# Two lanes of cells and queries that keep their results in DRAM, cross attention two sequences behind, inner products read from DRAM

## The chip, the cores and the metric

The kernel runs on one core of one Trainium2 chip. The metric is the device time in microseconds; the time of a kernel is the median of its runs. Less is better.

## The reference

Eight sequences of 512 tokens with 256 features go through two layers. Every `x = x + tanh(g) * f(layernorm(x))` is a stage. All arithmetic is float32.

```python
# _mlstm_cell: 8 heads of 32, gated and causal
log_D = where(tril, cs[:, :, None] - cs[:, None, :], -inf) + ig[:, None, :]
max_log_D = max(log_D, -1)
C = (q @ k.T) / sqrt(32) * exp(log_D - max_log_D)
h = (C / (maximum(abs(C.sum(-1)), exp(-max_log_D)) + EPS)) @ v
...
x = x + tanh(g_xattn[0]) * cell(layernorm(x), ctx, ctx)        # then layernorm(h) * ln_scale
x = x + tanh(g_ffn[0])   * block2(layernorm(x))                # 32 heads of 8, then 8 experts of 1024
x = x + tanh(g_xattn[1]) * cross(ctx, ctx, layernorm(x))       # 16 heads of 16
x = x + tanh(g_ffn[1])   * peer(layernorm(x))                  # product keys: 4096 experts, 8 of them per head
```

`block2` attends from all 512 tokens to all 512 (softmax), projects, adds, and sends fixed groups of tokens through their experts (gelu). `cross` attends from the sequence to its context. `peer` scores 2 x 64 sub-keys, takes the top 8 of the pairs, and weighs the chosen experts' `gelu(x . down)` by a softmax before the product with `up`. Its batch norm takes mean and variance over all tokens, so the scores of `peer` need every sequence to have passed cross attention.

## The kernel before

The kernel has two phases. `attention_phase` does cell, block 2 and cross attention for all sequences, and the inner products of all 4096 experts with seven of the eight sequences. What follows (`fold_phase` and the loop over `steps` at the end) does the product keys. The change is inside the attention phase.

The backbone of the attention phase is a list of 24 score jobs: for each place m in `order` two jobs of block 2, `("A", m, 0)` and `("A", m, 1)` with 16 heads each, and one of cross attention, `("C", m, 0)`. A job has 16 steps (4 groups of heads by 4 chunks of 128 tokens). It goes through the steps twice: first `maxima` computes queries by keys and takes the negated row maxima (L405, on DVE), which go as one more row into the queries' operand; then `exponentials` computes the transposed scores with the maxima already in, ACT takes the exponential (L433), and `values` multiplies by the value operand (L448). The loop at the end of the phase takes one step of the maxima of one job and one step of the exponentials of an earlier job together, where both are ready: the products of the two stand side by side in the program, on different rows of the array (L387). If one of the two isn't ready, the step is made with the other alone; if neither, the step is empty.

All else is side work in lanes, Python generators that yield either the cost in microseconds of the products that they have just issued, or a condition: `("wait", t)`, `("rest", event)`, `("take", True)` for the one shared accumulator bank (tag `ac`). `beside(credit)` is called twice a step and lets lanes issue until the credit is used up, in a fixed order of preference. So TensorE's order is the order in which this planner calls the instructions (it is set by hand for TensorE alone); the orders on DVE, ACT, GpSimd (POOL) and the sync engine's queue (SP) are made by the framework's scheduler from it.

```python
LAG, CREDIT, GROUP, RETURN = 2, (1.3, 2.4), 1.1, 2.6
jobs += [("A", m, 0), ("A", m, 1)]
if 0 < m < M - 2:
    jobs.append(("C", m - 1, 0))
lanes = [Lane(g()) for g in (between, after, before, behind, fill)]
```

The lanes: `before` runs `cell(m)` and `queries(m)` for all m in turn. A cell loads x into `qn` and the context into `cT` and `cte` (L515 to L518, DMAs issued by POOL), normalizes and transposes, makes the gates and their running sums in rows of 8 x 512, stores the running maximum to DRAM (`nM_d`, L562) and, for each of four pairs of heads, loads it back spread over all partitions (`mb`, L583), masks it (L591 on POOL), takes the exponential (L599, ACT) and multiplies scores (L621), decay (L626, DVE) and values (L606). `queries` projects queries and keys of block 2 and stores them to DRAM (`qk_d`). `between` spreads them into one of three operand sets (L357) and projects the values into `v0` in SBUF. `behind` does output projection, experts, operands and values of cross attention; `after` adds the cross attention, stores the stream and its transpose to DRAM (`x_d`, `xT_d`) and adds to the batch norm's Gram matrix; `fill` makes the inner products (L130), evacuates them (L921) and stores them (`h_d`).

Before, a cell can't begin until its predecessor's queries are done, the stream X of a sequence stands in SBUF from the cell on (three buffers), the values of block 2 can't be projected until `v0` is free, and a job set is given by its half: sets 0 and 1 to the halves, 2 to cross attention.

Of the kernel before, what the change touches and what calls it, by code (L numbers as in the profile page):

```python
# [10 lines left out]
F32 = mybir.dt.float32  # L11
# [10 lines left out]
P = 128  # L22
# [14 lines left out]
def kernel(  # L37
# [52 lines left out]
    def layernorm(dst, src, user):  # L90
# [3 lines left out]
        mv = small.tile([P, NC, 2], F32, name="ln_mv", tag=f"ln_mv{user}", bufs=4 if user == "x" else 1)  # L94
        rs = small.tile([P, NC], F32, name="ln_rs", tag=f"ln_rs{user}", bufs=4 if user == "x" else 1)
# [83 lines left out]
    def attention_phase(ctx: ExitStack):  # L179
# [5 lines left out]
        row = ctx.enter_context(tc.tile_pool(name="row", bufs=1))  # L185
# [17 lines left out]
        gw_sb = row.tile([P, 6, 16], F32, name="gw_sb", tag="cs")  # L203
# [86 lines left out]
        W0, W1, WC = 32 * 9 + 23, 16 * 17 + 15, 8 * 33 + 31  # L290
        v0 = cst.tile([P, NC, W0], F32, name="v0")
        v1 = cst.tile([P, NC, W1], F32, name="v1")
        cte = cst.tile([P, NC, WC], F32, name="cte")
        nc.gpsimd.memset(v0, 1.0)
# [6 lines left out]
        m_f = row.tile([B * NC, P], F32, name="m_f", tag="e")  # L301
# [73 lines left out]
        class Attention:  # L375
# [35 lines left out]
            def close_maxima(self):  # L411
# [6 lines left out]
                nm_sb = row.tile([16, S], F32, name="nm_sb", tag="e")  # L418
# [20 lines left out]
            def values(self):  # L439
# [6 lines left out]
                for j in range(4):  # L446
                    h = (64 * j + self.first) // self.hd + g
# [8 lines left out]
                if self.o is None:  # L456
                    self.o = outs[self.m].setdefault(
                        self.hd, None
                    ) or tok.tile([P, NC, D], F32, name="o", tag="o", bufs=2)
                    outs[self.m][self.hd] = self.o  # L460
# [24 lines left out]
        xbs, cTs, lnx, nTs, qks, xTs, weights = {}, {}, {}, {}, {}, {}, {}  # L485

        def load(m):

            b = order[m]
            xbs[m] = xbp.tile([P, NC, D + 1], F32, name="X")  # L490
            nc.gpsimd.dma_start(xbs[m][:, :, :D], x[b].rearrange("(c p) d -> p c d", p=P))
            nc.gpsimd.memset(xbs[m][:, :, D], 1.0)
            return xbs[m][:, :, :D]
# [6 lines left out]
        def load_expert(n):  # L500
# [3 lines left out]
            nc.gpsimd.dma_start(w1e, w1[e].rearrange("(k p) f -> p k f", p=P))  # L504
            w2e = wmp.tile([P, NF, D], F32, name="w2e", tag="w2e")
# [3 lines left out]
            weights[n] = (e, w1e, w2e, b2e)  # L509


        def cell(m):
            b = order[m]
            qn = trp.tile([P, NC, D], F32, name="qn", tag="t1")
            nc.gpsimd.dma_start(qn, x[b].rearrange("(c p) d -> p c d", p=P))  # L515
            cT = load_context(m, "cTc")
            for c in range(NC):
                nc.gpsimd.dma_start(  # L518
                    cte[:, c, : 8 * 33].rearrange("p (h e) -> p h e", e=33)[:, :, 0:32],
# [1075 lines left out]
```

## Time and profile before

| | |
|---|---|
| median of 3 runs | 4019.05 us (4013.78 to 4032.41) |
| the profiled execution's own time | 4021.59 us |
| its span, first to last instruction | 4019.8 us |
| mean granted TensorE clock | 0.953 |
| TensorE busy | 3602.8 us |
| VectorE, ScalarE, GpSimd busy | 2277.1, 1757.1, 604.4 us |
| first score maximum (L405) | at 156.6 us |
| end of attention, start of the product keys | about 3134 us |

The rows of the profile give busy times by engine; PE is TensorE's matmuls, PEld its weight loads, DVE the vector engine, ACT the scalar engine. A matmul row's duration is modelled, so a busy PE is not PE at its peak. The chain of waits is followed back from the last instruction. "sc" is the tile of scores of both kinds, told apart by the order of its operands: `sc<-ka,qa` are the maxima, `sc<-qa,ka` the exponentials.

### The profile page before, as it was taken

What the parts mean: (1) busy time and instruction counts of PE and PEld (TensorE: products, weight loads), DVE (VectorE), ACT (ScalarE), POOL (GpSimd) and SP (SyncE); (2) the same over time, 40 slices, a digit from 0 to 9 for tenths busy, and PEclk for the clock granted to TensorE, in tenths of its full rate; (3) what the DMA queues carried; (4) which work ended last, traced back from release to release, by engine and by line L of the source; (5) the groups of instructions that cost most, each with busy time, mean ns of one, the idle gap of its engine ahead of it and who ended that gap; (6) DMA issues with size and microseconds to landing.
All of it is one profiled execution on the core that took longest, in us unless ns stands there. A gap on an engine that the chain in (4) does not pass through costs nothing.

```text
span 4019.8 us, 75880 instructions
## 1 busy us (share of the span) xinstructions
PE 3602.8 (90%) x31049; PEld 1861.6 (46%) x31049; DVE 2277.1 (57%) x5581; ACT 1757.1 (44%) x2279; POOL 604.4 (15%) x611
## 2 busy tenths in 40 slices
PE   5587898889989999989998999878899899999998
PEld 2222243334334434433443443423444677777777
DVE  3455564555555555555645553455421679999993
ACT  2124454344544444444444434334344355555562
POOL 3210102011002002100200020010000123333331
PEclk7668999999999999999999999999899999999999
DMA  3201113123213312422232142110333353333331
GB/s 105 53 27 38 27 57 76 43 64 103 83 43 93 106 62 69 122 81 54 72 112 72 51 119 82 41 40 25 113 108 100 96 149 104 103 103 103 112 113 36
DMA packets 200392, 317.53 MB, mean 79 GB/s; under 512 B 24862, under 2 KB 153406, under 8 KB 191742
## 3 DMA queue, kind: packets, MB, share of 16 engines
q1 hardware_dynamic: 183564, 255.74, 21.5%
q0 software_dynamic: 15616, 56.63, 4.7%
q8 instruction: 244, 4.00, 0.4%
q14 instruction: 104, 0.85, 0.1%
q10 hardware_dynamic: 864, 0.32, 0.0%
HBM read 224.08 MB, written 87.72 MB: 78 GB/s over the span
## 4 chain that ended last, share of the span: by engine, by line
PE 78%; DVE 13%; issue 3%; ACT 2%; DMA 2%; POOL 1%; SPq 0%; DVEq 0%; POOLq 0%; ACTq 0%
PE sc L387 22%; PE acc L1437 11%; PE ps_hd L130 10%; DVE nm L405 9%; PE av L448 7%; PE cf L1417 3%; PE ps_y L764 3%; PE ps_sim L1169 3%; PE ps_q L347 3%; PE ps_p L336 3%; PE ps_h L747 3%; PE csc L621 2%; PE cav L606 2%; PE ps_t L317 1%; PE ps_hl L130 1%
## 5 line engine op out<-in xcount | busy, mean ns | idle before, releaser
L405 DVE TENSOR_REDUCE nm<-sc 128x2 f32<-128x1024 f32 x768 | 939.8, 1225 | 1024.6 <-PE sc L387 1021.0
L433 ACT ACTIVATE pr<-sc 128x1024 f32<-128x1024 f32 x768 | 785.8, 1024 | 1034.3 <-PE sc L387 1032.4
L387 PE MATMUL sc<-ka,qa 32*128 32x512 f32 x3072 | 940.8, 673 | 211.7 <-DVE nm L405 199.6
L387 PE MATMUL sc<-qa,ka 32*128 32x512 f32 x3072 | 895.0, 657 | 23.2 <-ACT pr L433 13.7
L387 PEld LDWEIGHTS sc<-ka,qa 32*128 32x128 f32 x3072 | 256.2, 191 | 624.8 <-DVE nm L405 430.6
L1437 PE MATMUL acc<-up_sb,gs 64*128 64x256 f32 x4096 | 468.3, 382 | 1.3 <-DVE gs L1426 1.3
L130 PE MATMUL ps_hd<-xT,dw 128*64 128x256 f32 x3584 | 432.5, 385 | 3.9 <-DVE pd L626 2.1
L448 PE MATMUL av<-pr,v 128*32 128x512 f32 x3072 | 427.3, 629 | 4.7 <-ACT pr L433 4.7
L1437 PEld LDWEIGHTS acc<-up_sb,gs 64*128 64x128 f32 x4096 | 389.8, 187 | 52.4 <-issue 4.7
L130 PEld LDWEIGHTS ps_hd<-xT,dw 128*64 128x64 f32 x3584 | 243.1, 137 | 232.2 <-issue 103.9
L1407 POOL TENSOR_TENSOR m<-o,cwT 128x1024 f32<-128x1024 bf16 x128 | 243.7, 1904 | 561.4 <-DVE o L1405 238.5
L387 PEld LDWEIGHTS sc<-qa,ka 32*128 32x128 f32 x3072 | 241.3, 187 | 68.2 <-issue 32.4
L921 ACT COPY hb<-ps_hd 128x512 f32<-128x512 f32 x224 | 130.9, 586 | 296.2 <-PE ps_hd L130 282.7
L599 ACT ACTIVATE pd<-mb,aT 128x512 f32<-128x512 f32 (+3 forms) x256 | 129.7, 553 | 211.0 <-PE cav L606 95.5
L448 PEld LDWEIGHTS av<-pr,v 128*32 128x32 f32 x3072 | 61.5, 109 | 308.9 <-issue 291.3
L591 POOL TENSOR_SCALAR_AFFINE_SELECT mb<-mb 128x256 f32<-128x256 f32 x128 | 52.4, 409 | 858.4 <-ACT pd L599 410.7
L1426 DVE TENSOR_TENSOR gs<-cf,gs 128x1024 f32<-128x1024 f32 x128 | 155.7, 1217 | 42.7 <-PE cf L1417 27.3
L626 DVE SCALAR_TENSOR_TENSOR pd<-csc,pd 128x512 f32<-128x512 f32 (+3 forms) x256 | 115.5, 485 | 96.0 <-PE csc L621 70.7
L621 PE MATMUL csc<-qT,cT 32*128 32x256 f32 (+3 forms) x512 | 148.1, 557 | 13.7 <-DVE pd L626 10.2
L1417 PE MATMUL cf<-m,m 64*64 64x64 f32 x8192 | 152.5, 221 | 0.8 <-DVE gs L1426 0.7
L1417 PEld LDWEIGHTS cf<-m,m 64*64 64x64 f32 x8192 | 134.8, 135 | 38.7 <-issue 38.3
L1403 ACT CAST m<-o 128x1024 f32<-128x1024 bf16 x128 | 133.6, 1044 | 39.2 <-DVE o L1401 35.4
(225 smaller groups left out, 4081.6 us busy)
## 6 DMA issues: line engine op xcount, KB each, us to landing
h_d<-hb SPq DMA_DIRECT2D x224, 256.0 KB
gs<-h_d SPq DMA_DIRECT2D x56, 1024.0 KB
dw<-in_down SPq DMA_DIRECT2D x112, 256.0 KB
w1e<-in_w POOLq DMA_DIRECT2D x16, 1024.0 KB, 5.4
w2e<-in_w POOLq DMA_DIRECT2D x16, 1024.0 KB, 6.4
mb<-nM_d SPq DMA_DIRECT2D x32, 512.0 KB
qk_d<-pk SPq DMA_DIRECT2D x64, 256.0 KB
ws<-in_w SPq DMA_DIRECT2D x56, 256.0 KB
```

The costliest lines, as they stand in the source:

```text
L130: nc.tensor.matmul(ps[64 * q : 64 * q + 64, :], dw[:, k, :], runs[:, :, q, :], start=(k == 0), stop=(k == NK - 1),)
L387: nc.tensor.matmul(sc[:, i, :], lhs[r : r + 32, g, c * P : (c + 1) * P], rhs[r : r + 32, g, :], start=True, stop=True,)
L405: newest = nc.vector.tensor_reduce(self.nm[:, c, 2 * half : 2 * half + 2, g], sc, AX.X, ALU.max, negate=True)
L433: nc.scalar.activation(self.pr[jj], sc, AF.Exp)
L448: nc.tensor.matmul(self.av[32 * j : 32 * j + 32, :], self.va[:, c, h * (self.hd + 1) : h * (self.hd + 1) + 32], pr[j // 2][:, j % 2, :], s ...
L621: nc.tensor.matmul(sc[i][:, s0:], cT[r : r + 32, g, s0 : s0 + P], qT[r : r + 32, g, s0:], start=True, stop=True,)
L921: nc.scalar.copy(hb.rearrange("p n i t -> p i n t"), ps.rearrange("p i (n t) -> p i n t", n=2),)
L1403: nc.scalar.copy(m1, o1)
L1407: nc.gpsimd.tensor_tensor(m2, o2, tokens(cw), ALU.mult)
L1417: nc.tensor.matmul(cf[64 * q : 64 * q + 64, h, s, :], m2[rows, 4 * q + s // 2, :, s % 2], m1[rows, 4 * q + s // 2, :, s % 2], start=True, ...
L1426: nc.vector.tensor_tensor(gv, cf.rearrange("p h s i -> p i h s"), gv, ALU.mult)
L1437: nc.tensor.matmul(accs[n][q], gs[n % 2][rows, i, :], up_sb[rows, i, :], start=(i == 0), stop=(i == 63),)
```

## The change

Seven things are changed together, all in the attention phase.

1. Cells and queries run in two lanes: one takes sequences 0, 2, 4, 5, 6, 7, the other 1 and 3. The second works in tiles lent by what is not yet in use (`Lent`: the experts' weights and hidden units, and until the first scores the accumulator bank `av`). Before the first scores, the cells' products use the score banks.
2. The cell's result goes to DRAM (`x_d1`), and `behind` loads it as X when its turn comes. The values of block 2 are projected at the end of `queries`, stored to DRAM (`v_d`), and loaded into one of two half-size `v0` before their job.
3. The gates' rows use the cell's tiles `pd` and `mb`; the pool `row` is gone.
4. The cross attention of m-2, not of m-1, stands among the jobs of m, between the two; the three operand sets rotate.
5. The expert weights w1 are loaded when the hidden units are done, w2 and b2 later, and the pause between experts is 3, not 20. The first expert is loaded when the second lane is through.
6. The inner products read the transpose from DRAM (`xT5`) and need no longer share a tile with `leave`.
7. The credits fall from (1.3, 2.4) to (1.1, 2.1).

The core of the diff:

```diff
+        class Tiles:
+            user = ""
...
+            def pair(self):
+                return cel.tile([P, 2, S], F32, name="pd")
+
+            def bank(self, name):
+                return ps_ac.tile([P, S], F32, name=name, tag="ac")
...
+        class Lent(Tiles):
+            user = "2"
+
+            def __init__(self):
+                self.pds = wmp.tile([P, 2, 2, S], F32, name="pd2", tag="heT")
+                self.more = wmp.tile([P, 2, NC, D], F32, name="mb2", tag="w2e")
+                self.cte = wmp.tile([P, NC, WC], F32, name="cte2", tag="w1e")
...
-        def cell(m):
+        def cell(m, own):
...
+                def banks():
+                    if newest:
+                        return [ps_m.tile([P, S], F32, name="csc", tag="m") for _ in range(2)]
+
+                    two = ps_sc.tile([P, 2, S], F32, name="csc2", tag="sc")
+                    return [two[:, i] for i in range(2)]
...
-            yield ("rest", ("left", m - 3))
-            Xb = load(m)
...
-            nc.gpsimd.tensor_tensor(Xb, Xb, hk, ALU.add)
+            nc.gpsimd.tensor_tensor(Xa, Xa, hk, ALU.add)
+            xds[m] = drm.tile([P, NC, D], F32, name="x_d1", bufs=M)
+            nc.sync.dma_start(xds[m], Xa)
...
+            vds[m] = drm.tile([P, 2, NC, 16 * 9], F32, name="v_d", bufs=M)
             w = weights1.get()
             for c in range(NC):
-                ps = project(w, nTs[m], c)
-                nc.any.tensor_copy(
-                    v0[:, c, : 32 * 9].rearrange("p (h e) -> p h e", e=9)[:, :, 0:8],
-                    ps.rearrange("p (h e) -> p h e", e=8),
+                ps = project(w, nT, c)
...
+                nc.sync.dma_start(
+                    vds[m][:, :, c], pk.rearrange("p (f n) -> p f n", f=2)
                 )
                 yield 1.0
+            rested.add(("v_d", m))
...
+        def begin(m):
+            for f in range(2):
+                i, last = block2_set(m, f)
+                yield ("rest", ("qk", m))
+                if last:
+                    yield ("rest", last)
+                for half, src in zip(sets[i], qks[m]):
+                    spread(half, src, 32 * f, 8)
+                blank(sets[i][0])
+                ready.add(("A", m, f))
+                yield ("rest", ("v_d", m))
+                yield ("rest", ("A", m - 1, f))
+                nc.sync.dma_start(v0[f][:, :, : 16 * 9], vds[m][:, f])
+                ready.add(("v0", m, f))
...
+                if 2 * m + i + 1 < 2 * M:
+                    load_first(2 * m + i + 1)
...
                 if i == 0:
-                    yield ("wait", 20)
+                    yield ("wait", 3)
...
         def inner(m):
             b = order[m]
+            xT = exp.tile([P, NK, S], F32, name="xT5", tag="xT5", bufs=1)
+            nc.sync.dma_start(xT, xT_d[:, :, b * S : (b + 1) * S])
+            yield ("wait", 4)
...
-        LAG, CREDIT, GROUP, RETURN = 2, (1.3, 2.4), 1.1, 2.6
+        LAG, CREDIT, GROUP, RETURN = 2, (1.1, 2.1), 1.1, 2.6
...
         for m in range(M):
-            jobs += [("A", m, 0), ("A", m, 1)]
-            if 0 < m < M - 2:
-                jobs.append(("C", m - 1, 0))
+            jobs.append(("A", m, 0))
+            if 1 < m < M - 1:
+                jobs.append(("C", m - 2, 0))
+            jobs.append(("A", m, 1))
...
+        def before(sequences, tiles):
+            own = tiles()
+            for m in sequences:
+                Xa = yield from cell(m, own)
+                yield from queries(m, own, Xa)
+            if tiles is Lent:
+                rested.add("lent")
+                load_first(0)
+                load_second(0)
...
-        lanes = [Lane(g()) for g in (between, after, before, behind, fill)]
+        lanes = [Lane(g()) for g in (between, after)]
+        lanes += [Lane(before((0, 2, *range(4, M)), Tiles)), Lane(behind()), Lane(before((1, 3), Lent))]
+        lanes.append(Lane(fill()))
...
                 if (
                     job not in closed or tick < closed[job] + LAG or value not in ready
-                    or not free
+                    or not free or ("v_d", 1) not in rested
                 ):
```

## The prediction

> **What bounds the kernel now.** I read the page's totals, then a table of busy time by stretch, then the chain of waits inside single stretches. From the page, section 1 and section 4:
>
> ```profile
> PE 3602.8 (90%) x31049; PEld 1861.6 (46%) x31049; DVE 2277.1 (57%) x5581; ACT 1757.1 (44%) x2279; POOL 604.4 (15%) x611
> PE 78%; DVE 13%; issue 3%; ACT 2%; DMA 2%; POOL 1%; SPq 0%; DVEq 0%; POOLq 0%; ACTq 0%
> ```
>
> TensorE bounds the whole, but 90% is a mean. The busy table, with stretches cut where the score jobs change hands (columns: stretch, length, busy time and instructions of PE, weight loads, DVE, ACT, POOL, granted PE clock, DMA share, GB/s):
>
> ```profile
> 0.00:157.00 157.00, 80.75 (x222) 36.43 (x223) 54.69 (x127) 27.43 (x49) 58.95 (x79) 0.67 0.32 92
> 157.00:264.00 107.00, 89.16 (x276) 32.59 (x274) 61.38 (x95) 22.96 (x42) 7.39 (x17) 0.60 0.12 29
> 264.00:504.00 240.00, 192.11 (x1089) 64.55 (x1088) 136.29 (x237) 96.51 (x125) 33.25 (x44) 0.88 0.12 33
> 504.00:768.00 264.00, 232.30 (x1295) 103.64 (x1292) 141.36 (x230) 114.62 (x139) 32.75 (x45) 0.97 0.23 62
> 1101.00:2409.00 1308.00, 1212.01 (x8036) 546.39 (x8032) 705.93 (x1127) 593.73 (x728) 161.57 (x215) 0.99 0.28 81
> 2649.00:2846.00 197.00, 160.06 (x1004) 61.91 (x1000) 100.75 (x122) 86.70 (x87) 6.16 (x8) 0.97 0.09 23
> 3005.00:3134.00 129.00, 124.95 (x862) 61.11 (x858) 17.32 (x49) 55.14 (x71) 3.50 (x6) 1.00 0.35 111
> 3134.00:4019.00 885.00, 854.52 (x13890) 663.13 (x13890) 725.05 (x3143) 457.40 (x677) 247.08 (x130) 0.99 0.33 101
> ```
>
> The reader is to see three things. From 1101 to 2409 PE is 93% busy at full clock: little to win except by taking work out of its steps. Up to 264 PE is 64% busy and that at 0.60 to 0.67 of its clock. And from 2649 to 2846 it has holes, because the side work has run out. After 3134 the product-key phase begins, which the diff does not touch: 885 us stay.
>
> What a step costs is in the chain of 2660 to 2680, where nothing but scores runs:
>
> ```profile
> 2666.32 1.21 PE sc L387 x8
> 2667.54 1.22 DVE nm L405
> 2668.75 0.04 issue
> 2668.80 1.21 PE sc L387 x8
> 2670.01 1.22 DVE nm L405
> ```
>
> Half a step is scores 1.21 plus the maximum 1.22 plus 0.04: 2.47 us, a step 4.94. PE's own part is 2 x 1.21 and 1.00 for the value product (a row "av L448 x8" of 1.00 in the chain): 3.42. A step with scores for the exponentials alone has "sc L387" 1.06 twice and the 1.00: 3.1 us. So a step that carries only one of the two kinds costs PE nearly as much as one with both, since the two kinds use different rows of the array side by side (`jj` and `1 - half` in `pair`).
>
> **What the Trainium skill says.** "TensorE: Matmul & The Clock Gate", Part 1: the clock is halved after an idle window of about 3.4 us and given back after a busy one. The trace agrees in part: half clock up to 264 where PE waits, full clock later; but from 200 to 240 PE counts as 94% busy (37.7 of 40 us) at 0.51. The same page, Part 2, has matmuls stay in program order: so a product waiting for a DMA stops all products behind it. The chain at 190 to 262 shows this, with "DMA mb<-nM_d" 3.75, 3.85 and 3.67 us on the path. "DMA: Bandwidth & Descriptors", section "Anatomy of one DMA", prices a transfer at 2.0 us + bytes / 436 kB per us; the trace's 256 KB store of qk_d took 2.69 us against 2.6 by that.
>
> **The change, part by part.** The order of the two built programs has the same 16,231 products; only names differ. So PE's work is the same, and what changes is where it stands. Counting steps in the order: before, 352 with both kinds, 64 with one; after, 362 and 44. The planner's side work is 1279 of its units in both, and a unit is a microsecond: 16 ps_hd products are 1.8 units and 1.88 us in the chain.
>
> *Start (to the first scores).* Before 157. Two expert weights of 1 MB no longer stand ahead of qn: it was issued at 17.41 and took 11.32; with two half-size v0 memsets, as before in sum 1.1, it goes at about 15.1 and should take the 4.6 of its row's median, to land near 20: -9. Two cells now run before the first scores. The second's gates, in order on ACT and DVE, +6. The pair loops took 62 us for four pairs (49 to 111), mostly in the latency PE to DVE to PE; eight in two interleaved lanes, +15 (0 if perfectly hidden, +38 if PE at half clock is their bound, since PE counts as over 90% busy from 60 to 110 even so). 169 us.
>
> *First job of scores alone (16 steps).* 107 us before for 2.0 side units a step at clock 0.60. After, 2.6 units: 16 x (2.2+2.6) = 77 us at full clock, 128 at 0.60. I take 110.
>
> *The next 64 steps, up to the first job of the third sequence (2.6 units each).* After, all carry both kinds. PE 3.42+2.61 = 6.03. Loss: from 1101 to 2409, 175 steps took 1308 us, 7.47 each, with 3.45 units: 3.42+3.45 = 6.87, so 0.60 is lost. Early steps lose more: 504 us for 73 steps at 2.19 units is 6.9 each, 1.3 above 5.61; part of this is the one-sided steps, which go. I take 7.0: 448 us.
>
> *The middle, 240 steps.* The credits fall from (1.3, 2.4) to (1.1, 2.1) and the order has 2.90 units a step, since the cells have run ahead and the inner products spread. 3.42+2.90+0.60 = 6.92; some steps get under the 1.5 that hides beside the maxima, so 7.0: 1680 us.
>
> *The end.* Before, 2409 to 3134 = 725 us for 102 working steps and 308 units; after, 86 steps and 299 units are left. 16 steps fewer of 4.94 to 7.47: -79 to -120, taken as -102 (5.9 for a step, 0.9 for each unit): 623 us.
>
> Sum 169+110+448+1680+623 = 3030 against 3134: -104.
>
> *Moved steps, taken inside the counts.* The cross attention of m-2 goes between the two jobs of m; with it the sets rotate, and each job finds its set freed a job (16 steps, over 100 us) ahead, as before. This, the shorter pause between experts (20 to 3) and the earlier load of w1 are what lets the order have fewer one-sided steps (64 to 44); a set filled late would leave such steps again, at 3.42 us each. w1's load waits on POOL for the last product that reads it, as before, now ahead of the GELU and not after the second product group, so what is behind it waits less.
>
> *Added DMAs, taken at nothing.* SP gets 63 more issues of 0.3 us (SPq L357 in the chain: 0.29 to 0.33), 19 us beside a queue that mostly waits. The 16 loads of v0 (295 KB, 2.7 by the page's price, 5.3 as "ka<-qk_d" in the trace) stand a job, some 105 us, ahead of use; uncovered they would cost 16 x 5.3 = 85. The seven xT loads before inner products (512 KB; the rows of cT, qn and X land in 4.4 to 5.0 us) follow the store by two ps_g groups (3.7 us) and a step (7 us), against 3 + 5 needed; uncovered 7 x 8 = 56. X's reload waits on POOL for x_d1's store (about 3 us), and the masks of mb and the cte loads queue behind it; it is issued only when an older X is free, long after the store, so I take nothing (8 x 3 = 24 uncovered). On POOL the six Xa and two other loads are 8 x 0.8, the 32 vk memsets 32 x 0.1 by the row of X's; behind them wait the masks of mb (0.41), ahead of ACT, but POOL is 12% busy in the middle. On ACT 64 half copies replace 32 of 374 ns: at most +12 us of 44% busy. A gain of these edits by themselves is excluded: they take nothing off PE.
>
> The profiled execution took 4021.6 (span 4019.8 and 1.8 around it): 3917.6; the runs' median is 2.5 under it: 3915.
>
> **Rivals.**
> *Clock stays low.* If the early stretches keep 0.67, 0.60 and 0.88: start 180, first job 135, next 386/0.88+38 = 477: +65, 3980. For it: 94% busy at 0.51. Against: two lanes leave fewer gaps of 3.4 us.
> *Clock rises.* Start 160, first job 90, next 64 x 6.6 = 422, -55; the middle at 6.92, -19: 3841.
> *It does not do what it says:* holes only move, and just the steps saved count: 10 x 3.42 = 34 us, 3985. For it: PE is 93% busy in the middle; against: 142 us idle up to 504 and 37 from 2649 to 2846, in places that the new order fills.
> *Slower: SP's queue.* The 16 loads of v0 wait on SP for the value products that last read v0, and the loads of mb and nM_d of two cell lanes queue behind; products in order then wait at csc. The page's waits of SP have such waits for PE of up to 43.5 us ("qa<-qk_d" behind sc). At 9.5 us for each of 16, +152: 4067. It decides from 104/16 = 6.5 us each; against it, these loads are placed after the step that frees v0.
>
> **How the numbers follow.** Main case 0.48, low clock 0.17, high clock 0.16, holes only moved 0.10, slower 0.09. The range 3845 to 3990 leaves out the slower case and the tails of the two clock cases. A measurement of this kernel can tell about 0.5%, 20 us, from no change. Faster by more 0.83, within 0.09, slower 0.08, with a quarter of the low-clock and holes cases counted as no change.
>
> **What would show it.** Right: the first scores near 169; fewer than 7.1 us a step in the middle with PE over 92%; 300 to 500 at clock over 0.9; product-key phase 885. Wrong: steps of 7.4 in the middle, waits of SP for PE ahead of mb loads, csc products waiting for mb, or the clock at 0.6 past 250.

## The result, and the profile after

The changed kernel took 3970.89 us (median of 4 runs, 3966.72 to 3975.46), the kernel before 4016.41 beside it: ratio 0.9879, 95% interval 0.9849 to 0.9909. Its profiled execution took 3974.63 with a span of 3972.8. So 46 us were won where 104 were forecast.

The page's section 1 and section 4 of the changed kernel:

```profile
PE 3616.3 (91%) x31049; PEld 1861.4 (47%) x31049; DVE 2277.6 (57%) x5591; ACT 1763.3 (44%) x2305; POOL 617.2 (16%) x653
PE 63%; DVE 8%; DMA 1%; ACT 1%; issue 1%; POOL 0%; SPq 0%; DVEq 0%; ACTq 0%; POOLq 0%
```

TensorE is busy longer than before (3602.8) in a shorter span, with as many instructions. The shares of the second line add up to 74%: the chain is followed back over a part of the span only, so its 8% of DVE can't be set against the 13% of before.

The busy table of the changed kernel, cut where the prediction's steps end (start, length, busy time and instructions of PE, weight loads, DVE, ACT, POOL, granted PE clock, DMA share, GB/s):

```profile
0.00:195.60 195.60, 121.86 (x394) 53.35 (x394) 89.67 (x224) 49.19 (x92) 74.10 (x109) 0.65 0.33 96
195.60:320.10 124.50, 111.14 (x314) 42.63 (x316) 70.61 (x120) 24.93 (x47) 10.37 (x23) 0.61 0.23 59
320.10:798.90 478.80, 416.27 (x2382) 167.65 (x2380) 292.33 (x518) 213.16 (x280) 89.59 (x126) 0.92 0.22 68
798.90:2449.90 1651.00, 1528.71 (x10276) 666.98 (x10278) 867.78 (x1264) 758.28 (x908) 167.91 (x230) 0.99 0.29 82
2449.90:3084.60 634.70, 579.17 (x3735) 264.28 (x3732) 231.90 (x324) 258.08 (x297) 28.58 (x36) 0.97 0.28 85
3084.60:3972.00 887.40, 859.17 (x13957) 666.52 (x13955) 725.26 (x3143) 459.64 (x681) 246.62 (x129) 0.99 0.33 102
```

The first two stretches run at 0.65 and 0.61 of the clock, as before (0.67 and 0.60), and are longer than before. The third is the prediction's next 64 steps, the fourth its middle: 240 steps from 799 to 2450, in which TensorE is 93% busy.

Where the gain is, TensorE's waits show (line, what was waited for, us in total, times, longest). Before:

```profile
PE sc L387 <- DVE nm L405: 200.5, 270, 2.3
```

After:

```profile
PE sc L388 <- DVE nm L406: 142.7, 226, 3.4
```

The scores wait 57.8 us less for the maximum that must read the bank ahead of them. TensorE's idle time in the attention phase as a whole fell from 386 to 327 us, so this wait is nearly all of it.

A step has two halves. In the first the value product (av) follows the scores; in the second only side work can. TensorE's timeline at 2651, where side work has run out, shows both kinds of wait, in brackets (rows of the other scores left out):

```profile
2651.37 0.59 PE L388 MATMUL sc<-qa,ka 32*128 32x512 f32 x1
2653.29 0.69 PE L388 MATMUL sc<-ka,qa 32*128 32x512 f32 x1 [1.33 <-DVE nm L406]
...
2653.84 0.59 PE L388 MATMUL sc<-qa,ka 32*128 32x512 f32 x1
2654.36 1.07 PE L449 MATMUL av<-pr,v 128*32 128x512 f32 x8
2655.76 0.69 PE L388 MATMUL sc<-ka,qa 32*128 32x512 f32 x1 [0.34 <-DVE nm L406]
```

By the chain, in which the maximum takes 1.22 us, a hand-over 0.04 and the value product 1.00, a first half without side work should cost 1.22 + 0.04 - 1.00 = 0.26 us of waiting, a second half 1.26; the timeline has 0.07 or 0.08 more for each, since it sets the ends of products a little earlier. By the order in which the program was built, the first half is empty of side work 142 times before and 146 after, the second 126 and 71 times: 4 x 0.26 - 55 x 1.26 = -68, against -57.8.

The traces allow a closer count. Each wait for the maximum can be sorted by what TensorE did between the scores that wait and the scores before them:

| between the scores | before: waits, us | after: waits, us |
|---|---|---|
| nothing | 85, 115.2 | 50, 66.3 |
| the value product alone | 116, 40.9 | 123, 44.0 |
| side work that was too short | 69, 44.5 | 53, 32.6 |

The halves with nothing in them lost 49 of the 58 us, at 1.33 to 1.36 us each. There are 35 fewer of these waits, not 55, as not every empty half of the built order ends in one. So the sum of -68 came near partly by chance: it counts too many of these waits, and leaves out those behind short side work, which fell by 12.

### The profile page after: what moved, and what is told of

Same layout as the page of the kernel before. It is cut to its first block, busy times and chain, and to the rows that moved or that the text cites. A ratio compares the mean times of both kernels' runs of the same rounds, so it can differ in the third digit from the quotient of the medians.

```text
span 3972.8 us, 76203 instructions
## 1 busy us (share of the span) xinstructions
PE 3616.3 (91%) x31049; PEld 1861.4 (47%) x31049; DVE 2277.6 (57%) x5591; ACT 1763.3 (44%) x2305; POOL 617.2 (16%) x653
## 4 chain that ended last, share of the span: by engine, by line
PE 63%; DVE 8%; DMA 1%; ACT 1%; issue 1%; POOL 0%; SPq 0%; DVEq 0%; ACTq 0%; POOLq 0%
PE sc L388 17%; PE acc L1563 11%; PE ps_hd L131 10%; DVE nm L406 6%; PE av L449 5%; PE cf L1543 3%; PE ps_sim L1295 3%; PE ps_y L870 2%; PE ps_q L348 2%; PE ps_h L851 2%; PE ps_p L337 2%; PE ps_hl L131 1%; PE ps_g L964 1%; PE ps_t L318 1%; PE ot L470 1%
## 5 line engine op out<-in xcount | busy, mean ns | idle before, releaser
L388 PE MATMUL sc<-ka,qa 32*128 32x512 f32 x3072 | 958.8, 673 | 162.5 <-DVE nm L406 141.4
L699 PE MATMUL csc<-qT,cT 32*128 32x384 f32 (+3 forms) x512 | 143.4, 580 | 13.8 <-DVE pd L704 7.4
```

The lines of the kernel that those rows point to most:

```text
L388: nc.tensor.matmul(sc[:, i, :], lhs[r : r + 32, g, c * P : (c + 1) * P], rhs[r : r + 32, g, :], start=True, stop=True,)
L699: nc.tensor.matmul(sc[i][:, s0:], cT[r : r + 32, g, s0 : s0 + P], qT[r : r + 32, g, s0:], start=True, stop=True,)
```

## The experiments

A ledger was drawn from each trace: the length of the attention phase is TensorE's busy time as it would be at full clock ("work"), what half clock adds ("clock": half of the time that it was busy at half clock), and its idle time. This takes every product to last twice as long at half clock, which holds roughly: the same 394 products of the start come out as 72 us of work in the changed kernel and as 80 in the kernel with cross attention one behind, where less of the start was at half clock. "One-sided" are steps with scores of one kind; "empty" are half steps without side work, first and second halves, both counted in the built order; "wait" is the wait for the maximum. "Staggered" is the second of its two sets of runs.

| kernel | ratio to before (95%) | one-sided | empty | work + clock + idle, us | wait, us |
|---|---|---|---|---|---|
| before | 1 | 64 | 142, 126 | 2601 + 147 + 386 = 3134 | 200.5 |
| changed | 0.9879 (0.9849 to 0.9909) | 44 | 146, 71 | 2592 + 165 + 327 = 3084 | 142.7 |
| one lane | 1.0004 (0.9990 to 1.0017) | 74 | 141, 72 | 2622 + 166 + 342 = 3130 | 124.0 |
| old credits | 0.9968 (0.9952 to 0.9984) | 40 | 136, 92 | 2588 + 156 + 373 = 3117 | 164.5 |
| cross one behind | 1.0120 (1.0072 to 1.0169) | 68 | 171, 89 | 2620 + 165 + 385 = 3170 | 176.3 |
| credits alone | 1.0090 (1.0058 to 1.0122) | 98 | 158, 87 | 2640 + 139 + 378 = 3157 | 161.2 |
| lanes alone | 1.0187 (1.0157 to 1.0217) | 46 | 167, 110 | 2593 + 205 + 421 = 3219 | 184.3 |
| order alone | 1.0051 (1.0029 to 1.0074) | 64 | 140, 117 | 2612 + 166 + 385 = 3163 | 170.8 |
| one lane, (1.3, 1.7) | 0.9851 (0.9825 to 0.9877) | 72 | 100, 57 | 2615 + 164 + 299 = 3078 | 107.7 |
| staggered | 0.9827 (0.9805 to 0.9848) | 44 | 149, 63 | 2597 + 146 + 317 = 3060 | 142.6 |
| staggered, (1.1, 1.9) | 0.9808 (0.9789 to 0.9827) | 42 | 118, 47 | 2602 + 130 + 313 = 3045 | 126.2 |
| staggered, (1.3, 1.7) | 0.9790 (0.9763 to 0.9818) | 40 | 92, 61 | 2595 + 161 + 305 = 3061 | 135.4 |
| staggered, (1.0, 2.3) | 0.9822 (0.9797 to 0.9848) | 44 | 164, 76 | 2599 + 148 + 326 = 3073 | 154.5 |
| staggered, (0.6, 2.4) | 0.9973 (0.9959 to 0.9987) | 42 | 218, 52 | 2584 + 168 + 364 = 3116 | 150.2 |
| staggered, (1.9, 1.3) | 0.9941 (0.9920 to 0.9962) | 42 | 64, 117 | 2600 + 133 + 362 = 3095 | 188.1 |

### One lane

With no second lane there is nothing to wait for before the first expert's weights are loaded:

```diff
         def behind():
-            yield ("rest", "lent")
+            load_first(0)
+            load_second(0)
+            yield ("wait", 0)
...
-        lanes += [Lane(before((0, 2, *range(4, M)), Tiles)), Lane(behind()), Lane(before((1, 3), Lent))]
+        lanes += [Lane(before(range(M), Tiles)), Lane(behind())]
```

> The changed kernel with the second lane taken away: one lane runs all cells and queries in turn; all else of the change stays. Its order has 74 one-sided steps (44 in the changed kernel) and starts the scores after one cell. Theory (the two lanes are bound by a half-clock TensorE at the start, but the work they do there is saved later): the first scores near 160 us in place of 195.6, and 30 steps more of 3.4 to 5 us plus a fuller middle later, so slower than the changed kernel by 20 to 70 us: 3990 to 4040. Rival (the second lane costs at the start what it brings later): within 15 us of the changed kernel.

Measured 4024.33, within the theory, with the first scores at 143.5 where it had 160. The gain was gone: the start was 52 us shorter, but with 30 more one-sided steps 30 us of work came back, and the idle time rose by 15. At these credits the gain needs the second lane. Its empty halves are as many as the changed kernel's (141 and 72), and its wait for the maximum is the shorter one, 124.0 us. So fewer empty halves alone did not bring the gain: they pay for one wait, and work, half clock and the other waits can take it back.

### Old credits

```diff
-        LAG, CREDIT, GROUP, RETURN = 2, (1.1, 2.1), 1.1, 2.6
+        LAG, CREDIT, GROUP, RETURN = 2, (1.3, 2.4), 1.1, 2.6
```

> The changed kernel with the credits put back to (1.3, 2.4). 40 one-sided steps in place of 44, 440 steps in place of 444, more side work a step in the middle (and less left for the end). Theory (a loaded step costs TensorE's own 3.42 us plus the side units plus some 0.55): the sum of the work is the same, so within 20 us of the changed kernel, from 3955 to 3990. Rival (the smaller credit is what brings the gain): back to 4010 or more.

Measured 4011.19, the rival's side. With four one-sided steps fewer than the changed kernel it took 40 us more; idle time rose by 46, 22 of it at the maximum. So the number of one-sided steps doesn't tell the whole time.

### Warm start

Unread products behind the score products of the first two cells, 24 in all:

```diff
+                    if m < 2 and c < NC - 1:
+                        for _ in range(1):
+                            warm = ps_m.tile([P, S], F32, name="warm", tag="m")
+                            nc.tensor.matmul(warm, ident, qT[:, 0, :], start=True, stop=True)
```

> The changed kernel with 24 products added whose results nobody reads: one dense 128x128 by 512 product behind each csc pair of the first two cells but the last chunk, in the gap in which TensorE waits for VectorE. Theory (the start is long because the clock stays at half although TensorE counts as busy): the added products bring the clock to full, the pair loops shrink from some 93 us to 60 to 75, first scores at 165 to 180 in place of 195.6, and 15 to 30 us less in all. Rival (the start waits for DMAs and for the chain of engines, the clock is beside the point): first scores at 195 to 215, no gain or up to 20 us slower.

Measured 3963.89 (ratio 0.9839, 0.9806 to 0.9872), first scores at 187.0: between the two, and the interval overlaps the changed kernel's. TensorE was busy at half clock for 23 us of the start instead of 100, which is worth 38 us; the work of the start rose by 33. These products lifted the clock, but cost about what they gave. Why they lifted it, by filling gaps or by being products of 128 rows and not of 32, is not told apart.

### Staggered

```diff
+            if tiles is Lent:
+                yield ("wait", 40)
```

> The changed kernel, the second lane held back by 40 planner units, so that the first cell's normalization and gates don't stand behind the second's on GpSimd, ScalarE and VectorE. The order has the same 444 steps, 22+22 one-sided. Theory (about 9 us were lost because the second cell's loads and statistics stand ahead of the first cell's power on GpSimd, 31 us of the rest to the half clock): first scores at 180 to 192, 5 to 15 us less in all. Rival (the pair loops at half clock bound the start whatever stands ahead): first scores within 5 us of 195.6 and no change beyond 5 us.

Measured 3952.77 (0.9813, 0.9774 to 0.9852), first scores at 178.3, just ahead of the theory. What the trace shows for it is GpSimd's order. The changed kernel's timeline, its GpSimd rows and the first cell's statistics on DVE (start, length, line, operation; in brackets the idle time before it):

```profile
20.36 1.10 POOL L552 MEMSET cte<- 128x1180 f32 x1
20.39 1.41 DVE L98 BATCH_NORM_STATS2 ln_st<-qn 128x6 f32<-128x256 f32 x4 [3.90 <-DMA qn<-in_x]
...
22.84 3.55 POOL L592 DMA_DIRECT2D cte<-in_cx  x4
...
26.41 0.26 POOL L103 TENSOR_SCALAR ln_rs<-ln_mv 128x4 f32<-128x4 f32 x1
29.71 0.22 POOL L103 TENSOR_SCALAR ln_rs<-ln_mv 128x4 f32<-128x4 f32 x1 [3.03 <-DVE ln_mv L102]
29.93 0.81 POOL L741 DMA_DIRECT2D Xa<-in_x  x1
30.76 2.04 POOL L104 TENSOR_TENSOR ln_rs<-ln_rs,eps 128x4 f32<-128x4 f32 x2
```

The first cell's statistics begin at 20.4 us, 8.4 earlier than before (28.8). But GpSimd then issues the second cell's loads (22.84), and only behind them, at 26.41, does the first part of the first cell's power (L103) run. Its second part (L104) stands behind the second cell's L103, which waits for that cell's data, and behind the load of Xa: 30.76. So the transposes begin at 32.3 us and not 8.4 us ahead of the 33.1 of before. With the stagger they begin at 27.45. TensorE's idle time to the first scores was 74 us in the changed kernel and 59 here. GpSimd's order alone, without the stagger, was not tried, and the stagger also moves the second cell's other work.

### Staggered and warm

The stagger, and unread bf16 products by an identity, four ahead of each of 24 score groups of the first two cells and four in each half step of the first job (224 in all: the expectation below counts too few groups):

```diff
+                        for _ in range(4):
+                            nc.tensor.matmul(warm, identb, oneb.to_broadcast([P, S]), start=True, stop=True)
```

> The changed kernel with the second lane starting 40 planner units late (as in the staggered run, 3953 us) and, on top, products that nobody reads, bf16 of 128x128x512, four before each of the eight csc score groups of the first two cells and four in each half step of the first score job (160 in all; bank av is free then). Theory (the early misses are largely the half clock, which dense products lift): the half-clock time up to the first job's end falls by 80 us or more, the first scores start at 150 to 170 instead of 178, the first job takes 80 to 98 us instead of 105, and the whole 3905 to 3940. Rival (the clock follows something else than how full TensorE is, or the loss is waiting and not clock): half-clock time and both stretches within 8 us of the staggered run, and the whole 3945 to 3985, by the time the extra products take.

Measured 3954.99 (0.9831, 0.9798 to 0.9863). The busy table of this kernel, start and first job (columns as above):

```profile
0.00:175.30 175.30, 120.49 (x486) 49.45 (x495) 84.15 (x211) 51.53 (x96) 69.61 (x103) 0.87 0.35 102
175.30:286.00 110.70, 104.49 (x414) 39.97 (x424) 69.09 (x117) 20.12 (x40) 15.96 (x27) 0.90 0.26 74
```

The clock went to 0.87 and 0.90, and half-clock time up to the first job's end fell from 177 us (staggered) to 68, as the theory said. But the first scores came at 175.3 and not at 150 to 170, the first job took 110.7 us and not 80 to 98, and the whole is the staggered version's, on the rival's side. The unread products were busy for 66 us. The half clock of the early stretches can thus be lifted, but in neither of these two trials for less than it costs.

### Cross attention one behind

```diff
-            jobs.append(("A", m, 0))
-            if 1 < m < M - 1:
-                jobs.append(("C", m - 2, 0))
-            jobs.append(("A", m, 1))
+            jobs += [("A", m, 0), ("A", m, 1)]
+            if 0 < m < M - 2:
+                jobs.append(("C", m - 1, 0))
```

(with the sets and places of o that go with it)

> The changed kernel with one part undone: the cross attention goes again one sequence behind and after both score jobs of a sequence, with the sets of rows and the places of o as before; lanes, results in DRAM, credits and inner products as changed. The order has 68 one-sided steps instead of 44 (the kernel before has 64). Theory (each one-sided step saved is worth about 2.5 to 3.5 us, as the length of the attention phase is its steps): 24 steps more, 4025 to 4060, slower than the kernel before. Rival (only the lanes and the smaller credit matter and the holes just move): 3960 to 3990.

Measured 4062.77, just past the theory's 4060: 92 us above the changed kernel, of which work is 28 and idle time 58.

### Inner products from SBUF

```diff
+            if m:
+                yield ("rest", ("H", m - 1))
...
-            xT = exp.tile([P, NK, S], F32, name="xT5", tag="xT5", bufs=1)
-            nc.sync.dma_start(xT, xT_d[:, :, b * S : (b + 1) * S])
-            yield ("wait", 4)
```

> The changed kernel with one part undone: the inner products read the transposed stream from the SBUF tile again instead of fetching it from DRAM, so the next sequence's leave step waits for them (as before); the rest as changed. The order keeps its 44 one-sided steps, the planner's end is 34 units later, with more side work after the last scores. Theory (what matters is that there is side work for every step; holding it back leaves steps unfilled early and work over at the end): 3985 to 4010. Rival (steps are bound by the chain of scores and maxima, the placing of inner products is free): 3960 to 3980.

Measured 3965.27 (0.9856, 0.9821 to 0.9890): the rival. This part of the change is worth nothing that can be measured, either way.

### Credits alone

The kernel before with one line changed:

```diff
-        LAG, CREDIT, GROUP, RETURN = 2, (1.3, 2.4), 1.1, 2.6
+        LAG, CREDIT, GROUP, RETURN = 2, (1.1, 2.1), 1.1, 2.6
```

> The kernel before with one part alone: the credits (1.1, 2.1) in place of (1.3, 2.4). The order has 98 one-sided steps instead of 64, since the cells come too late. Theory (the smaller credit is worth 40 us only once the lanes have put the side work far enough ahead; without them it starves): 4030 to 4090, slower than before. Rival (it is worth the same 40 us by itself, less work wedged between a score and its maximum): 3975 to 3995.

Measured 4056.83, as the theory said: slower. The cells come too late, 34 more one-sided steps, 39 us of work.

### Lanes alone, order alone

The kernel with cross attention one behind, and the one with one lane, each with the old credits:

```diff
-        LAG, CREDIT, GROUP, RETURN = 2, (1.1, 2.1), 1.1, 2.6
+        LAG, CREDIT, GROUP, RETURN = 2, (1.3, 2.4), 1.1, 2.6
```

> The kernel before with only the two lanes and the results in DRAM: the cross attention one sequence behind as before, the credits (1.3, 2.4) as before. The order has 46 one-sided steps and 407 steps in all; with the small credit it had 68 and 418 (4063 us). From the runs so far a working step past the first 80 costs some 4.6 us, with one kind of scores or both, and a unit of side work 0.8 us. Theory (steps are what the parts buy, and a large credit goes with the old place of the cross attention): 11 steps less than with the small credit, 4000 to 4020. Rival (the place of the cross attention costs by itself, whatever the credit): 4040 to 4065.

> The kernel before with only the cross attention two sequences behind (its sets and places of o, results in DRAM): one lane of cells, credits (1.3, 2.4). The order has 64 one-sided steps and 416 in all, as many as the kernel before (64 and 416). Theory (a part is worth the steps that it saves): as the kernel before, 4005 to 4030. Rival (the place by itself takes waits out of the middle): 3975 to 4000.

Measured 4101.27 and 4043.95. Both theories fell, and both rivals: each was slower than any case foreseen. The lanes alone have 46 one-sided steps, about as few as the changed kernel, and lost 78 us to the kernel before. Their waits:

```profile
PE sc L388 <- DVE nm L406: 184.3, 270, 2.6
```

110 empty second halves instead of 71, 42 us more of this wait than in the changed kernel, 94 us more idle time in all and 40 us more of half clock; the first scores came at 203.7 and nothing won the start back. So none of the three parts is a gain alone: credits, order and lanes were slower by 0.9, 0.5 and 1.9%, and of the pairs only lanes with order came out ahead, by 0.3%. Each of the three waits less for the maximum than the kernel before (161.2, 170.8 and 184.3 us for 200.5) and was slower all the same.

### Less credit, and the changed kernel again

```diff
-        LAG, CREDIT, GROUP, RETURN = 2, (1.1, 2.1), 1.1, 2.6
+        LAG, CREDIT, GROUP, RETURN = 2, (1.1, 1.9), 1.1, 2.6
```

> The staggered version (second lane 40 units late, 3953 us) with the second credit lowered once more, (1.1, 1.9) for (1.1, 2.1). The order has 405 steps, 42 of them one-sided, against 406 and 44. Theory (less side work wedged into a step is less waiting, as long as no step is added): 3930 to 3948. Rival (the work only moves behind the last scores): 3950 to 3975.

> The changed kernel itself once more, for a second profile of its start. Three kernels with nearly the same products up to the first scores took 174.6, 182.4 and 195.6 us to them, at 77, 100 and 141 us of half clock in the first 200. Theory (the clock in the start differs from execution to execution, and the 195.6 of the first profile was a late one): first scores at 172 to 190 this time or again up to 198, in step with the half-clock time, and the whole 3960 to 3976. Rival (the start is fixed by the program): 195 to 197 again, with 135 to 145 us of half clock.

The staggered version with (1.1, 1.9) took 3945.54, within the theory, but its interval overlaps the staggered one's. The changed kernel took 3965.33 (0.9856, 0.9834 to 0.9878), with the first scores at 194.1 and 143 us of half clock, nearer to the rival. Start of the kernel with cross attention one behind, with the same count of products to the first scores:

```profile
0.00:174.60 174.60, 94.77 (x394) 43.53 (x394) 89.07 (x224) 49.18 (x92) 74.01 (x109) 0.84 0.35 107
```

and of the changed kernel's second profile:

```profile
0.00:194.10 194.10, 121.25 (x394) 53.07 (x394) 89.39 (x223) 49.36 (x92) 74.01 (x109) 0.65 0.33 96
```

DVE, ACT and GpSimd have the same busy times, TensorE is busy 26 us longer at 0.65 than at 0.84. The start took 174.6, 182.4, 194.1, 195.6, 197.7 and 203.7 us in the six profiles of kernels that differ only after it or in the credits. The staggered kernel's two profiles, of one and the same program, differ too:

```profile
0.00:178.30 178.30, 118.95 (x398) 53.34 (x398) 83.19 (x209) 51.76 (x96) 70.03 (x103) 0.69 0.35 100
0.00:174.30 174.30, 113.92 (x398) 51.79 (x398) 83.21 (x210) 51.68 (x96) 68.46 (x103) 0.73 0.37 103
```

In the first 200 us they were at half clock for 131 and 116 us. So a part of the start's clock is not fixed by the program; how large it is, and what decides the rest, stays open. The Trainium skill, "TensorE: Matmul & The Clock Gate", Part 1, says that the windows in which activity is judged run freely, whatever the kernel does. These two profiles would fit that, while the changed kernel's two came out alike; no run here shows the windows themselves.

### Few and many empty half steps

The staggered version with other credits, (1.3, 1.7) and (1.0, 2.3), the one-lane kernel with (1.3, 1.7), and the staggered version again:

```diff
-        LAG, CREDIT, GROUP, RETURN = 2, (1.1, 2.1), 1.1, 2.6
+        LAG, CREDIT, GROUP, RETURN = 2, (1.3, 1.7), 1.1, 2.6
```

> The staggered version with the credits (1.3, 1.7) for (1.1, 2.1). Nearly the same number of half steps, 808 for 812, but 153 of them without any side work in the built order where the staggered one has 212. Over the eleven kernels so far, PE's waits of the scores for the maximum (200.5 us at 268 empty half steps before, 142.7 at 217 after) rise by 0.67 us for each empty half step. Theory (empty half steps are what the change saves): these waits 95 to 118 us and the whole 3910 to 3938, below the staggered version run beside it by 15 to 40. Rival (the empties only go with something else, and what a credit saves at one wait it wedges in at another): waits lower, but the whole within 10 us of the staggered version.

> The staggered version with the credits (1.0, 2.3) for (1.1, 2.1): 812 half steps as there, but 240 without side work instead of 212. Theory: waits of the scores for the maximum 150 to 172 us, the whole 12 to 35 us above the staggered version run beside it. Rival: within 10 us of it.

> The changed kernel with one lane of cells (as the one-lane run, 4024 us: 842 half steps, 213 empty) and the credits (1.3, 1.7): 840 half steps, 157 empty. Theory (empties decide, lanes are only one way to fewer of them): 3970 to 4000, so most of the gain of the change without its second lane. Rival (the lanes are needed for the one-sided steps that they save, 44 for 74): 4010 to 4035.

> The staggered version itself again, as the measure for the two above on the same chip and for its start: theory (the stagger takes 15 to 20 us of TensorE's idle time out of the start; 74, 73, 80 and 80 without it, 59, 55 and 59 with it): idle time to the first scores 52 to 63 us, whole 3943 to 3960; rival (chance): idle 70 to 82.

Measured 3944.21, 3955.00, 3966.24 and 3957.94. With one lane it went as the theory had it, and 4 us below its range: 58 us less than at (1.1, 2.1), so other credits put as large a gain as the change's (0.9851 for 0.9879 and 0.9856) into a kernel with one lane and 72 one-sided steps. The kernel before was not tried with (1.3, 1.7), so how much of the gain credits alone could bring is open. With two lanes the theory failed: waits of 135.4 us for the expected 95 to 118, and a whole 14 below the staggered version, intervals overlapping; with many empties the wait was as expected (154.5), but the whole was the same, as the rival had it. So the total count of empties is not the cause either. What the staggered version showed of the start came again: 60 us of idle time, as expected.

### First and second halves

```diff
-        LAG, CREDIT, GROUP, RETURN = 2, (1.1, 2.1), 1.1, 2.6
+        LAG, CREDIT, GROUP, RETURN = 2, (0.6, 2.4), 1.1, 2.6
```

and (1.9, 1.3).

> The staggered version with the credits (0.6, 2.4). The order has 405 steps, 42 one-sided (staggered version: 406, 44), and 270 half steps without side work, 218 of them the first of a step and 52 the second (staggered: 149 and 63). Theory (the value product of 1.00 us stands in the first half, so an empty first half leaves 1.22 + 0.04 - 1.00 = 0.26 us of waiting for the maximum, an empty second half 1.26): waits of the scores for the maximum 142 + 69 x 0.26 - 11 x 1.26 = 146 us, 138 to 155; the whole within 15 us of the staggered version (3953 and 3958). Rival (empties count alike, 0.67 us each): 142 + 58 x 0.67 = 181 us, the whole 25 to 50 above it.

> The staggered version with the credits (1.9, 1.3): again 405 steps, 42 one-sided, but 181 half steps without side work, 64 first and 117 second ones. Theory: waits of the scores for the maximum 142 - 85 x 0.26 + 54 x 1.26 = 188 us, 172 to 196; the whole 25 to 55 us above the staggered version, 3980 to 4010. Rival (empties count alike): 142 - 31 x 0.67 = 121 us, the whole at or below the staggered version, 3930 to 3957.

Waits of the kernel with empty first halves:

```profile
PE sc L388 <- DVE nm L406: 150.2, 257, 4.4
PE sc L388 <- ACT pr L434: 30.8, 16, 8.5
PE ht L719 <- DVE avs L716: 28.5, 21, 2.2
PE ps_p L337 <- DVE pd L704: 15.5, 5, 11.2
```

and of the kernel with empty second halves:

```profile
PE sc L388 <- DVE nm L406: 188.1, 235, 4.8
```

The wait for the maximum was 150.2 us where 146 was worked out, and 188.1 where 188 was; counting empties alike would have given 181 and 121. The first kernel has more empties in all (270 for 181) and less wait: which half is empty decides. Sorted as above, waits with nothing between the scores took 64.0 us in the first kernel and 119.9 in the second, against 70.0 in the staggered version; those behind the value product alone 70.3 and 20.8, against 43.4. The prices of 0.26 and 1.26 us held here for the difference from the staggered version. They don't give the wait by themselves: over the fifteen kernels of the table the measured wait lies between 13 us below and 36 above 0.26 for each empty first half and 1.26 for each second. The whole of the second kernel, 3989.94, was within the theory; its ledger has 45 us more idle time than the staggered version's, which is this wait, and 13 less of half clock. The whole of the first, 4010.69, was not: 53 us above the staggered version, nearer to the rival's 25 to 50, where the wait explains 8. Half clock adds 22, less work takes off 13, and the rest are other waits. Up to 2.4 units of side work now stand in a row in one half; that products of a cell or a projection then wait for their own evacuation is the likely reason, and not tested. Between 200 and 3045 us the waits of side products for DVE are 100 us here and 59 in the staggered version, those of the scores for ACT 31 and 20.

## Why the prediction was wrong

Direction and range were right, and so was the picture that the change moves work and hardly saves any (2592 us of work for 2601). The gain was mis-sized, 46 us for 104. In the sum by stretch, 3030 was forecast to the end of attention and 3085 measured (the second profile: 3088).

*Start: 169 forecast, 195.6 measured.* The step that failed is "eight in two interleaved lanes, +15 (0 if perfectly hidden, +38 if PE at half clock is their bound)". By the ledger the start was 48 + 32 + 76 (work, clock, idle) before and is 72 + 50 + 74 after: the second cell's products are 24 us of work and 18 of half clock, and the idle time hardly changed. So hardly anything of the second cell was hidden, and the term's upper bound was about the case. The prediction's own reading, over 90% busy at half clock from 60 to 110, had left no room to hide it in. The term "-9" failed too: the load did land near 20, but the first cell's normalization waited in GpSimd's order behind the second's loads. "+6" for the second gates is not seen apart from these. A part of the miss is the clock of this start, which took 174.6 us in another kernel with the same 394 products.

*First job: 110 forecast, 124.5 measured.* 67 us of work (77 were counted), 44 of half clock, 13 idle: the clock stayed at 0.61 where the forecast had taken the middle.

*Next 64 steps: 448 forecast, 479 measured, the largest miss.* The work, 384 us, is that of the forecast (64 x 6.03 = 386). The step that failed is the loss, "I take 7.0", which left 0.97 us a step for it: it is 1.5, 33 us of half clock, of which the forecast had none, and 63 idle.

*Middle: 1680 forecast, 1651 measured.* Work 1509 us is 6.29 a step, where 3.42 + 2.90 = 6.32 was said; loss 0.59 where 0.60 was said. The sum of 6.92 was right (6.88) and should not have been rounded up to 7.0.

*End: 623 forecast, 635 measured*, with 56 us idle. Product-key phase 885 forecast; 887.4 in the table to the end of the span.

The work was thus right to 8 us in the two long stretches for which it was given; +27, +14, +31, -29 and +12 are the 55 us. That the whole stayed in the range is in part luck: the rounding in the middle gave back 29 us of the 84 that the other four missed.

The rival "clock stays low" had 180, 135 and 477 for the first three, 792 together; 799 was measured. It was the nearest case, with 3980 for 3971. But its 477 is luck: it has 53 us of half clock and 38 of other loss, and measured were 33 and 63. And lifting the clock by unread products took as long as it gave.

"It does not do what it says" counted 10 steps of 3.42, 34 us; the work fell by 9. One-sided steps show in the work (30 more in the one-lane kernel, 30 us more), but didn't tell the whole time. SP's queue, the slower rival, is not seen: no wait of a csc product is put down to a load of mb, and the waits of the scores for a DMA are single ones of up to 8.3 us. Of the DMAs taken at nothing, the xT5 loads were tested: without them the time is the same. The loads of v0 were not, but in the changed kernel no value product is seen to wait for one. The price of a DMA that the prediction took from the Trainium skill, "DMA: Bandwidth & Descriptors", section "Anatomy of one DMA", is given there for transfers issued by GpSimd. The prediction used it for SP's, and of its two rows for these the store agrees, 2.69 us against 2.6, while the load ka<-qk_d has 5.3.

For what brought the gain the prediction had no term of its own. It counted steps, with such waits inside a mean loss for each; the time came off the wait for the maximum, 58 us of the 59 us by which idle time fell, and 49 of these in halves with nothing beside the maximum. That such halves cost this much was then shown by making more of them: 50 us more of these waits, and 32 us more in all (0.9941 for 0.9827). That fewer of them are enough for a gain is not so: the kernel with one lane has as few as the changed kernel and no gain. So lanes, order and credits together gave it: by the ledger fewer such halves and no more work, while half clock took back 18 us. What remains open: which other credits would do for the kernel before, why the first of the two kernels of the last trial lost 39 us in other waits, and what sets the clock of the start.

The staggered version with credits (1.3, 1.7) or (1.1, 1.9) beats both kernels: 0.9790 (0.9763 to 0.9818) and 0.9808 (0.9789 to 0.9827), against 0.9856 (0.9834 to 0.9878) of the changed kernel's second set of runs.

## What to carry to other kernels

In a loop of product, reduction and product, look for the half steps that have nothing to put beside the reduction, and price each by what the chain shows to be uncovered there. That tells one wait. The time is this wait, the other waits, the work and the clock together, and here a kernel that waited 76 us less for its maxima than the one before was no faster. A count of steps saved, or an average over a stretch, tells less. Parts of such a change don't add up: each of three parts was slower alone. When work is moved ahead into a stretch where TensorE runs at half clock and is over 90% busy, as here, don't count on its being hidden.

## What was not expected of the hardware

TensorE stayed at half clock for 130 us in a row (48.5 to 178.3 in the changed kernel's start). It counts as busy for 75% of them, and for 93% of the 60 us from 80 to 140. 24 unread products of 128x512 cut the time that it was busy at half clock in the start from 100 us to 23. The same first 394 products went with 77 us of half clock in the first 200 us in one profile and with 141 in another, and took 174.6 against 195.6 us to the first scores.
